# Window sums kept in one range of 128 PSUM columns, two windows to a bank, in a graph layer on one core

## The chip, the core and the metric

The kernel runs on one core of a Trainium2 chip. The core has a matmul engine (PE; its weight loads appear as PEld), a vector engine (DVE), a scalar engine (ACT), GpSimd (POOL) and SyncE (SP), which issues most of the DMAs. They work side by side, each through its own list of instructions in order, and wait for each other by semaphores. Matmuls write into PSUM, which has eight banks of 512 float32 columns for each of 128 partitions; DVE and ACT read it from there. The metric is the device time of one execution in microseconds, lower is better.

## The reference

A graph layer with a residual and a layer norm over 6250 nodes of 128 features and 100,000 edges that are sorted by destination:

```python
Xs = X[src]
m_data = Xs @ W_data.T + b_data
m_ctrl = Xs @ W_control.T + b_control
msg = jnp.where((edge_types == 0)[:, None], m_data, m_ctrl)
agg = jax.ops.segment_sum(msg, dst, num_segments=X.shape[0])
out = jax.nn.relu(agg + (X @ W_self.T + b_self))
x = layernorm(x + out)          # per node, eps 1e-5
```

Source and destination of an edge are random; on average 16 edges end in a node.

## The kernel before

**The table.** A message depends on the source node and the edge type alone. So the kernel first computes both products for all nodes: 49 blocks of 128 nodes times two types give 98 tables of 128 rows. The float32 values are split into three bfloat16 parts whose sum is nearly exact, side by side in 384 columns (`m3`, 128 x 98 x 384). This runs in 25 steps of two blocks (lines 485 to 520): a bias matmul (L499), two float32 matmuls (L502), ACT writes the first part (L507), a matmul with minus the identity takes it out of PSUM (L510), ACT or DVE writes the second part (`evict`), and DVE subtracts to get the third (L514). The blocks of transposed x come by DMA (`load_x`, L479); seven steps are loaded ahead, the others after the first part of an earlier step. `m3` is also stored to DRAM as `table`.

**The windows.** The first 6240 nodes are 39 windows of 160. A window's edges lie close together in the sorted list. A group of windows (one, two, then nine times four) is prepared in `ranks`: its edges are loaded, each edge gets a place in a list of slots, sorted by table (L702 to L779), and the lists go through DRAM (`packed`) and come back as a broadcast over 128 partitions (`rows`, L927). To find an edge's rank within its table, triangular matmuls write into a PSUM bank named `rk` (L713, L738; `ga` for the first group), and DVE takes the maximum of each row (L744). There is one such bank, so PE and DVE take turns in it.

**The sums.** `sums` then does for each window 25 groups of four tables. Stage one (L956): DVE has turned the list into 0/1 columns (L935), and four matmuls, each on 32 columns of the array, fetch 32 messages from each table: a bank `g` of 128 slots by 384 columns, with three banks in turn. ACT or DVE casts it to bfloat16 (`gs`, L444 or L445). Stage two (L970, L973): a 0/1 matrix `hot2` (DVE, L943) maps the 128 slots to the 160 nodes of the window. Four matmuls over 384 columns add the three parts, still side by side, into `a[:, :384]` for the first 128 nodes; three more, over 128 columns each, one for each part, add the other 32 nodes into `a[:, 384:]`, on three different ranges of 32 partitions. `a` has two banks. In group 12 the nodes' own product is added (`own`, L527, L530). At the end of a window ACT reads the last 128 columns (`bs`), and DVE adds the three ranges of 384 columns into `s` (L570).

**The end.** `close` adds x after the ReLU (L579) and does the layer norm for a group of windows. The ten nodes that are left are done by `gathered`: two indirect DMAs on POOL fetch their rows of `table`, and matmuls sum them in the bank `ga`.

**The order.** It is written out by a planner (`Plan`): each operation has an engine, or two to choose from, a planned duration (`act(cols)`, `dve(cols)`, constants for PE), a due time, and what it reads and writes. `Plan.run` goes through time and gives each free engine the ready operation that is due first; the instructions are then issued in that order. Buffers of one name form a ring: a user of the next buffer waits for all users of the one that it takes over. The planner's times only fix the order; on the chip semaphores decide.

PSUM before: `vt` 1 bank, `rk` 1, `ga` 1, `a` 2, `g` 3.

## Time and profile before

| | |
|---|---|
| time, median of 3 runs | 645.41 us (641.18 to 647.32) |
| profiled execution | 644.74 us, span 642.9 us |
| PE busy | 555.6 us, 86%, 13810 matmuls, 13810 weight loads |
| DVE busy | 496.3 us, 77% |
| ACT busy | 487.6 us, 76% |
| POOL busy | 31.3 us, 5% |
| mean DMA rate | 100 GB/s |

A row of the groups gives line, engine, operation, output <- input with shapes, the count (x), then the busy time in us and the mean of one in ns, and the idle time of the engine just before with what ended it. A row of a timeline gives start and length in us; in square brackets stands the idle time before it and what ended it. "issue" is a wait for nothing that the profile shows. A row of the waits gives the total in us, the count and the longest. A row of the stretches gives the stretch, its length, the busy time and the count of instructions of an engine, the granted clock, the share of the DMA engines and GB/s. A row of the DMA queues gives packets, MB, and the time of the packets as a share of 16 DMA engines' time.

### The profile page before, as it was taken

How to read it: one execution, taken by the hardware profiler on the slowest of the kernel's cores; microseconds unless marked ns; L12 is line 12 of the kernel's file. 1: busy time of each engine (PE TensorE's matmuls, PEld its weight loads, DVE VectorE, ACT ScalarE, POOL GpSimd, SP SyncE). 2: the span in 40 equal slices, each digit the busy share in tenths (PEclk: the TensorE clock that was granted, in tenths of full speed). 3: DMA queues.
4: the chain of work that ended last, by engine and by line, in shares of the span. 5: the costliest groups of instructions: out<-in, count | busy, mean ns of one | idle time of the engine just before them, and what ended most of it. 6: DMA issues, size and time to landing. Idle time of an engine off the chain costs nothing.

```text
span 642.9 us, 32170 instructions
## 1 busy us (share of the span) xinstructions
PE 555.6 (86%) x13810; PEld 427.6 (67%) x13810; DVE 496.3 (77%) x1502; ACT 487.6 (76%) x1258; POOL 31.3 (5%) x32
## 2 busy tenths in 40 slices
PE   5878789459989989898998899889889988989992
PEld 3544567338868777776787687678768767766771
DVE  6679688948988898788699979879987988685411
ACT  3545678348879787787888788888889788778992
POOL 1000100100010001001000100100010010010000
PEclk9989899759999999999999999999999999999997
DMA  3895821162045105403520630351253054022300
GB/s 109 244 303 160 246 58 50 22 188 80 3 125 153 44 33 181 107 6 125 135 63 29 188 106 4 125 165 32 73 147 94 5 185 104 17 90 95 82 16 15
DMA packets 56060, 64.33 MB, mean 100 GB/s; under 512 B 18159, under 2 KB 47828, under 8 KB 55908
## 3 DMA queue, kind: packets, MB, share of 16 engines
q1 hardware_dynamic: 54417, 59.68, 31.0%
q0 software_dynamic: 1120, 2.23, 1.6%
q8 instruction: 110, 1.80, 1.2%
q14 instruction: 43, 0.34, 0.2%
q10 hardware_dynamic: 370, 0.26, 0.2%
HBM read 45.94 MB, written 14.30 MB: 94 GB/s over the span
## 4 chain that ended last, share of the span: by engine, by line
PE 68%; ACT 12%; DVE 7%; DMA 5%; issue 5%; SPq 1%; another core or an unknown queue 0%; ACTq 0%; POOLq 0%; DVEq 0%
PE a L970 24%; PE g L956 23%; ACT gs L444 7%; PE rk L738 5%; PE a L973 5%; PE vt L775 3%; ACT to_d L451 3%; DMA hots<-past 2%; PE rk L713 1%; DVE slot L744 1%; PE g L502 1%; PE a L527 1%; DMA rows<-packed 1%; DVE rows L935 1%; PE vt L862 1%
## 5 line engine op out<-in xcount | busy, mean ns | idle before, releaser
L444 ACT CAST gs<-g 128x384 bf16<-128x384 f32 x927 | 391.8, 483 | 85.4 <-PE g L956 69.1
L956 PE MATMUL g<-m,rows 128*32 128x384 bf16 x3822 | 364.1, 331 | 14.0 <-DVE rows L935 8.4
L970 PE MATMUL a<-gs,hot 128*32 128x384 bf16 x3744 | 341.8, 333 | 34.1 <-ACT gs L444 21.0
L956 PEld LDWEIGHTS <-rows 128*32 128x32 bf16 x3822 | 250.4, 134 | 26.5 <-DVE rows L935 9.5
L970 PEld LDWEIGHTS <-hot 128*32 128x32 bf16 x3900 | 172.7, 95 | 103.7 <-issue 61.9
L973 PE MATMUL a<-gs,hot 128*32 128x128 bf16 x2808 | 231.9, 220 | 0.3 <-issue 0.3
L744 DVE TENSOR_REDUCE slot<-rk 124x4 f32<-124x392 f32 x209 | 117.4, 562 | 49.3 <-PE rk L738 42.8
L973 PEld LDWEIGHTS <-hot 128*32 128x32 bf16 x2925 | 116.7, 97 | 8.4 <-issue 4.6
L943 DVE TENSOR_TENSOR hot<-iota_b,to_d 128x1280 bf16<-128x1280 bf16 (+1 forms) x117 | 95.7, 841 | 0.0
L738 PE MATMUL rk<-hots,tri 128*32 128x392 bf16 (+1 forms) x880 | 86.1, 324 | 9.5 <-DMA hots<-past 5.3
L702 DVE TENSOR_TENSOR hots<-iota_b,st 124x784 bf16<-124x784 bf16 (+2 forms) x120 | 58.6, 506 | 4.9 <-PE vt L775 4.9
L935 DVE TENSOR_SCALAR rows<-rows,pid 128x1568 bf16<-128x1568 bf16 x78 | 46.9, 622 | 16.2 <-DMA rows<-packed 16.1
L738 PEld LDWEIGHTS <-tri 128*32 128x32 bf16 x968 | 38.4, 96 | 18.6 <-issue 13.5
L884 POOL DMA_INDIRECT sr<-table,at x20 | 25.9, 1293 | 476.4 <-DVE to_d L877 425.6
L570 DVE TENSOR_REDUCE s<-a 128x128 f32<-128x384 f32 x39 | 21.7, 556 | 34.6 <-PE a L973 22.9
L775 PEld LDWEIGHTS <-two 124*64 124x64 bf16 x858 | 21.7, 110 | 12.2 <-DVE two L766 5.9
L775 PE MATMUL vt<-hots,two 124*64 124x98 bf16 x836 | 26.1, 210 | 3.4 <-DVE two L766 1.7
L451 ACT COPY to_d<-vs 32x100 bf16<-32x100 bf16 (+3 forms) x84 | 22.2, 265 | 1.3
L760 DVE TENSOR_TENSOR hr<-slot_f,slot 124x768 bf16<-124x768 bf16 (+2 forms) x39 | 20.2, 517 | 2.6 <-ACT slot L448 2.6
L444 ACT CAST gl<-g 64x384 bf16<-64x384 f32 x39 | 18.4, 472 | 4.7 <-PE g L956 4.7
L713 PE MATMUL rk<-hots,later 124*32 124x392 bf16 (+1 forms) x210 | 20.8, 335 | 0.8 <-DVE slot L744 0.8
L766 DVE TENSOR_TENSOR two<-hr,lo 124x768 bf16<-124x768 bf16 (+2 forms) x39 | 20.2, 517 | 0.1
(188 smaller groups left out, 502.1 us busy)
## 6 DMA issues: line engine op xcount, KB each, us to landing
rows<-packed SPq DMA_DIRECT2D x39, 784.0 KB
table<-m SPq DMA_DIRECT2D x12, 768.0 KB
xc<-in_xt SPq DMA_DIRECT2D x9, 320.0 KB
rows<-in_xt SPq DMA_DIRECT2D x8, 256.0 KB
xr<-in_x SPq DMA_DIRECT2D x8, 256.0 KB
out<-xr SPq DMA_DIRECT2D x8, 256.0 KB
gl<-sr SPq DMA_DIRECT2D x39, 48.0 KB
win<-in_edges SPq DMA_DIRECT2D x38, 32.0 KB
```

The costliest lines, as they stand in the source:

```text
L444: [("ACT", act(cols), lambda: A.copy(o(), src())), ("DVE", dve(cols), lambda: V.tensor_copy(o(), src()))], None, None, due, r, w, lat)
L451: "ACT", 0.1 + cols / 1000, lambda: A.copy(o(), src()), due, r, w)
L702: lambda k=k, kn=kn, ci=ci, hs4=hs4: V.tensor_tensor(hv(ci)[:EP, k - KS[ci] : k - KS[ci] + kn].rearrange("p k w (c d) -> p (k w) c d", d=2 ...
L713: T.matmul(cnt.t[R * j : R * j + R, :wide], later.t[:EP, R - 1 - k : 2 * R - 1 - k], flat(k, EP), start=k < 4, stop=k + 4 > KT - 2, skip_g ...
L738: T.matmul(acc.t[R * j : R * j + R, (k - k0) * wide : (k - k0 + 1) * wide], tri.t[:, R * j : R * j + R], flat(k, P), start=k == k0, stop=True,
L744: vec(due, (k1 - k0) * wide, lambda k0=k0, k1=k1, acc=acc: V.tensor_reduce(slot.t[:, k0:k1, :], acc.t[:EP, : (k1 - k0) * wide].rearrange(" ...
L775: T.matmul(vv()[q : q + 64, i // 2, :], two.t[:EP, (k - k0) * nw + i].rearrange("p f r -> p (f r)"), one(k)[:EP, i, :], start=k == 0 and i ...
L935: add("DVE", dve(half * NT, 0.335), lambda sp=sp, rs=rs: V.tensor_scalar(sp.t[:, rs], sp.t[:, rs], pid1.t, None, op0=ALU.is_equal), due - ...
L943: lambda i=i, hot2=hot2, s4=s4, c0=c0, c1=c1: V.tensor_tensor(hot2.t[:, c0:c1].rearrange("p g (c d) -> p g c d", d=2), iota1_b.t.rearrange ...
L956: T.matmul(gp.t[R * t : R * t + R, :D3], sp.t[:, :, 4 * g + t], m3.t[:, 4 * g + t, :], start=True, stop=True)
L970: T.matmul(a.t[R * j : R * j + R, :D3], hot2.t[:, g, R * j : R * j + R], gs.t, start=g == 0, stop=False, skip_group_check=True)
L973: T.matmul(a.t[R * c : R * c + R, D3:], hot2.t[:, g, P:], gs.t[:, c * D : (c + 1) * D], start=False, stop=last, skip_group_check=True)
```

## The change

The three parts of a window's sum are added in the same 128 columns: stage two has twelve matmuls over 128 columns (three parts times four ranges of 32 nodes) and the three for the other 32 nodes as before. A sum now takes 256 columns, and two windows share one bank, `ab` (class `Half`). [...] `close` feeds the sum straight from PSUM to the ReLU step; the reduction into `s` stays for the ten gathered nodes alone.

The banks that are freed go to `rk`, which has two and serves the first group and the gathered nodes too, and to `g`, which has four. The table's products use `g` alone. In every second step of the table the third part comes from a second matmul with minus the identity and an eviction, not from DVE's subtraction, and the second part is always ACT's. All loads of x are issued without waiting for a step. The gathered nodes are planned 260 planned us later. Planned durations of ACT and of some matmuls change.

PSUM after: `vt` 1 bank, `rk` 2, `ab` 1, `g` 4.

```diff
+class Half(Buf):
+    @property
+    def t(self):
+        return self.base.t[:, self.turn]
...
             for i, b in enumerate(ring):
+                b.turn = i % b.bufs
...
 def act(cols):
-    return 0.055 + cols / 1200
+    return 0.12 + cols * 0.00085
...
+    banks = Buf(plan, ps, [P, 2, 256], F32, "ab", 1)
+    turn = Buf(plan, None, None, None, "turn")
+
+    def sums_bank():
+        b = Half(plan, None, None, None, "a", 2)
+        b.base = banks
+        return b
...
-    G0, G1 = 0.0, -4
+    G0 = 20
...
-    def load_x(q, after):
+    def load_x(q):
         if q in loads:
             c, i, j, q0 = loads[q]
             add("SP", SPD, lambda: S.dma_start(
                 xf(c)[:, i * P : j * P], xt[:, q0 * P : (q0 + j - i) * P]),
-                4.0 + MS * q - 9, after, [(xts[c], i)], lat=3.0)
-    AHEAD = 7
-    for q in range(AHEAD):
-        load_x(q, [])
+                -9.0 + 0.5 * q, [], [(xts[c], i)], lat=3.0 + 0.6 * q)
+    for q in range(NS):
+        load_x(q)
...
-        mp = B(ps, [P, 512], F32, *(("a", 2) if q % 5 > 2 else ("g", 3)))
+        mp, half = B(ps, [P, 512], F32, "g", 4), 0
...
-            add("PE", 0.5 if i else 0.71, product, due + 0.5 * i, [xk, w_sb, one3, brows], [mp])
+            add("PE", 0.43 if i else 0.64, product, due + 0.5 * i, [xk, w_sb, one3, brows], [key])
...
-        evict(lambda mv3=mv3: mv3(1), pv3, n, due + 1.8, [mp], [(m3, (q, 1))])
-        add("DVE", dve(n), lambda pv3=pv3, mv3=mv3: V.tensor_sub(mv3(2), pv3(), mv3(1)),
-            due + 2.4, [mp, (m3, (q, 1))], [(m3, (q, 2))])
+        add("ACT", act(n), lambda pv3=pv3, mv3=mv3: A.copy(mv3(1), pv3()), due + 1.8, [key],
+            [(m3, (q, 1))])
+        if q % LOP:
+            add("DVE", dve(n), lambda pv3=pv3, mv3=mv3: V.tensor_sub(mv3(2), pv3(), mv3(1)),
+                due + 2.4, [key, (m3, (q, 1))], [(m3, (q, 2))])
+        else:
+            add("PE", 0.11 * nb, lambda f=less_part: f(1), due + 2.4, [minus, (m3, (q, 1))], [key])
+            evict(lambda mv3=mv3: mv3(2), pv3, n, due + 3, [key], [(m3, (q, 2))])
...
-                s = B(work, [P, D], F32, "s", 3)
-                vec(da, D3 + 70, lambda a=a, s=s, m=m: V.tensor_reduce(
...
+                got, src = a, lambda a=a, m=m: a.t[:m, :D]
+                if tag:
+                    s = B(work, [P, D], F32, "s", 1)
...
-        bank = "rk" if gi else "ga"
-        cnt = B(ps, [P, 512], F32, bank, 1)
+        cnt = B(ps, [P, 512], F32, "rk", 2)
...
-            acc = B(ps, [P, 512], F32, bank, 1)
+            acc = B(ps, [P, 512], F32, "rk", 2)
...
-            a = B(ps, [P, 512], F32, "a", 2)
+            a = sums_bank()
...
-                gp = B(ps, [P, 512], F32, "g", 3)
+                gp = B(ps, [P, 512], F32, "g", 4)
...
-                    for j in range(4):
-                        T.matmul(a.t[R * j : R * j + R, :D3], hot2.t[:, g, R * j : R * j + R],
-                                 gs.t, start=g == 0, stop=False, skip_group_check=True)
                     for c in range(3):
-                        T.matmul(a.t[R * c : R * c + R, D3:], hot2.t[:, g, P:],
+                        for j in range(4):
+                            T.matmul(a.t[R * j : R * j + R, :D], hot2.t[:, g, R * j : R * j + R],
+                                     gs.t[:, c * D : (c + 1) * D], start=g == 0 and c == 0,
+                                     stop=False, skip_group_check=True)
+                    for c in range(3):
+                        T.matmul(a.t[R * c : R * c + R, D:], hot2.t[:, g, P:],
                                  gs.t[:, c * D : (c + 1) * D], start=False, stop=last,
                                  skip_group_check=True)
-                add("PE", 0.22, stage2, d + 0.9, [gs, (hot2, (g >= 9) + (g >= 17))], [a])
+                add("PE", 0.23, stage2, d + 0.9, [gs, (hot2, (g >= 9) + (g >= 17))] + (
+                    [turn] if g else []), [a] if g else [a, turn])
...
-            ga = B(ps, [P, 512], F32, "ga", 1)
+            ga = B(ps, [P, 512], F32, "rk", 2)
...
-    g0, g1 = T0 + G0, T0 + (NW + G1) * TW
-    step = max((g1 - g0) / max(sum(GT), 20), GC + 0.02)
+    g0, step = T0 + G0 * TW, GC + 0.02
```

## The prediction

> **What bounds the kernel now.** I read the page first: the busy times, the DMA queues and the chain that ended last.

> ```profile
> PE 555.6 (86%) x13810; PEld 427.6 (67%) x13810; DVE 496.3 (77%) x1502; ACT 487.6 (76%) x1258; POOL 31.3 (5%) x32
> q8 instruction: 110, 1.80, 1.2%
> PE 68%; ACT 12%; DVE 7%; DMA 5%; issue 5%; SPq 1%; another core or an unknown queue 0%; ACTq 0%; POOLq 0%; DVEq 0%
> ```

> PE carries two thirds of the chain; ACT and DVE are busy nearly as long. To see where a window's time goes I split the span at the reads of the window sums: window 3 is read at 151.70 us, window 38, the last, at 629.7. After that read and the group of all of them come the matmuls (x) in the stretch before it and in the middle, then the waits of the middle.

> ```profile
> 151.70 0.56 DVE L570 TENSOR_REDUCE s<-a 128x128 f32<-128x384 f32 x1
> L570 DVE TENSOR_REDUCE s<-a x39: 547/558/559, 89.8 to 629.7; 128x128 f32<-128x384 f32 x39
> 61.00:151.70 90.70, 67.59 (x1517) 0.83 0.37 103
> 151.70:629.70 478.00, 438.93 (x11871) 1.00 0.30 87
> ACT gs L444 <- PE g L956: 53.1, 67, 3.0
> DVE slot L744 <- PE rk L738: 34.3, 47, 1.5
> PE a L970 <- ACT gs L444: 17.4, 38, 1.5
> PE a L970 <- issue: 7.2, 8, 1.3
> PE vt L775 <- issue: 1.7, 1, 1.7
> ```

> The middle is 35 windows in 478.0 us, 13.66 each, with PE busy 92% of it. Each window runs 11871/35 = 339 matmuls, each with its own weight load (equal counts on the page). Next the timeline inside a dense stretch:

> ```profile
> 301.60 0.35 PE L970 MATMUL a<-gs,hot 128*32 128x384 bf16 x4
> 301.76 0.24 PE L973 MATMUL a<-gs,hot 128*32 128x128 bf16 x3
> 301.78 0.38 PE L956 MATMUL g<-m,rows 128*32 128x384 bf16 x4
> 301.99 0.35 PE L970 MATMUL a<-gs,hot 128*32 128x384 bf16 x4
> ```

> One group of slots takes 0.39 us: 11 matmuls and 11 weight loads. Then the waits "issue", in which PE waits for no semaphore. Two of them in the timeline, the matmul counts between four such stalls (211.53, 269.01, 311.12, 545.94), and the instruction queue in windows of 0.1 us at 266.8, 270.1, 308.8 and 312.3:

> ```profile
> 269.01 0.41 PE L775 MATMUL vt<-hots,two 124*64 124x98 bf16 x9 [1.66 <-issue]
> 311.12 0.32 PE L956 MATMUL g<-m,rows 128*32 128x384 bf16 x1 [0.84 <-issue]
> 211.53:269.01 57.48, 51.86 (x1408) 1.00 0.31 91
> 269.01:311.11 42.10, 37.94 (x1023) 1.00 0.29 89
> 311.12:545.94 234.82, 216.64 (x5886) 1.00 0.32 94
> q8 instruction: 1, 0.02, 60.1%
> q8 instruction: 1, 0.02, 87.9%
> q8 instruction: 1, 0.02, 60.9%
> q8 instruction: 1, 0.02, 89.8%
> 305.45:311.11 5.66, 3.63 (x129) 1.00 0.79 230
> ```

> So a block cannot follow the one before it faster than 1.2 (asking) + 1.12 (the mean packet: 1.2% x 16 x 642.9 / 110) + 1.25 (landing to running) = **3.6 us**. Now a dense block takes 128/11 x 0.39 = 4.5 us and the mean block of the middle 478/(11871/128) = 5.15 us. The fetch is hidden, with under 1 us to spare where PE is dense.

> **The change, part by part.** *The sum in one range of 128 columns.* For each group, four matmuls over 384 columns become twelve over 128; the three over 128 stay. Streaming is the same: a quarter of PE's array (32 of its columns) still runs 384 + 128 columns. What is added is 8 matmuls and 8 weight loads in each of 25 groups, 200 pairs for a window. Would the array keep up? The nearest row is the scatter:

> ```profile
> 324.34 0.71 PE L775 MATMUL vt<-hots,two 124*64 124x98 bf16 x24
> 324.98 0.35 PE L970 MATMUL a<-gs,hot 128*32 128x384 bf16 x4
> ```

> 24 matmuls of 98 columns, each with a weight load, in two halves of the array: 0.64 us, 27 ns each with the start, so 53 ns per half for 98 columns (41 ns of streaming at the pace of 384 columns in 0.16 us). Weight loads hide there, and a group costs 0.39 to 0.40 us in the array as before. But 19 pairs in 0.39 us use up a block of 128 pairs in 2.6 us, and it takes 3.6 us to bring one. Per window: (339 + 200)/128 = 4.21 blocks, at 3.6 us 15.2 us against 13.66 now.

> To that come late packets. The middle stretch has 11871/128 = 93 blocks and nine exposed stalls in the rows above; the late packet lost 3.3 - 1.2 = 2.1 us. If only those nine were late, 0.2 us per block. If the broadcast that each window needs holds one of its 4.2 blocks each time, 0.5:

> ```profile
> rows<-packed SPq DMA_DIRECT2D x39, 784.0 KB
> ```

> I take 0.4, nearer to the second, since a denser PE asks more often while a broadcast runs: a block every 4.0 us, 16.8 us per window.

> The stalls put borders at 256 instructions and show a wait one block after a late packet. [...]

> *The bank shared by two windows.* The reads of one window's sum now share a bank with PE's writes of the next. In before two reads of one bank, of different columns, stand behind one another:

> ```profile
> 618.00 0.56 DVE L570 TENSOR_REDUCE s<-a 128x128 f32<-128x384 f32 x1 [7.60 <-PE a L973]
> 618.59 0.26 ACT L444 COPY bs<-a 96x128 f32<-96x128 f32 x1 [0.27 <-DVE s L570]
> L579 DVE SCALAR_TENSOR_TENSOR xr<-s,xr 128x128 f32<-128x128 f32 x39 | 11.1, 284 | 0.1
> L579 DVE SCALAR_TENSOR_TENSOR xr<-vt,xr 128x128 f32<-128x128 f32 (+1 forms) x10 | 2.9, 286 | 0.2
> L943 DVE TENSOR_TENSOR hot<-iota_b,to_d 128x1280 bf16<-128x1280 bf16 (+1 forms) x117 | 95.7, 841 | 0.0
> ```

> ACT waits for DVE although neither writes. So I expect PE's next second-stage matmuls to wait for both reads: 0.26 + 0.29 us and three hand-overs of 0.03, less a first stage of 0.16 that can go between, about 0.5 us a window; 1.3 if DVE is in one of its 0.84 us masks. Behind the waiting matmul stand the first stages and rank products; ACT's evictions and DVE's slot maxima wait for those. The block time covers it: PE needs 2.6 of each 3.6 us. Without that cover it costs 18 to 45 us in all.

> *The reduction goes.* 39 x 0.556 = 21.7 us leave DVE; the ReLU step reads PSUM at the same price (284 against 286 ns). DVE is not what ends a window, so I count 0.3 us at the last one. A half is now held until the rows of x are there; they are asked for 20 us ahead.

> *Four slot banks, two rank banks, new planner costs.*

> ```profile
> L444 ACT CAST gs<-g 128x384 bf16<-128x384 f32 x927 | 391.8, 483 | 85.4 <-PE g L956 69.1
> ```

> They attack the three waits above: at most (53.1 + 34.3 + 17.4)/35 = 3.0 us per window, on three engines at once. While blocks arrive every 4 us they are not what is late, so nothing. ACT being priced dearer moves more evictions to DVE, 0.48 us each on ACT, into the time freed there.

> *The lead-in.*

> ```profile
> 24.65 0.16 DVE L1010 TENSOR_TENSOR t_rel<-t_raw,gbase 128x2 f32<-128x2 int32 x1 [3.80 <-DMA t_raw<-in_edges]
> 44.21 0.52 PE L738 MATMUL rk<-hots,tri 128*32 128x196 bf16 x8 [3.42 <-DMA hots<-past]
> 127.32 9.65 DMA hots<-past
> L514 DVE TENSOR_TENSOR m<-g,m 128x512 bf16<-128x512 f32 x15 | 10.3, 685 | 4.3 <-ACT m L444 4.3
> ```

> The gathered nodes move 260 planned us later with all they issue: the load and the two gathers on POOL's queue (POOL is busy 31.3 us in all), SP's loads and store, small DVE steps with one mask and one reduction, two matmuls and the own product. The 3.8 us stall of DVE goes; in the window loop those steps lie beside PE. All loads of x go out first on SP; four of them now stand ahead of the first window's edges. 13 of 25 third parts go from DVE (0.69 us) to a PE matmul and an eviction; the table's products get four banks instead of five. The first window starts 0 to 6 us sooner. What really holds window 3 is the ranks of its group, whose chain ends in the 9.65 us DMA. A second rank bank shortens it; PE's slower blocks lengthen it: windows 0 to 2 and the ranks ran 1517 pairs up to 151.7, now 2300, 18 blocks or 72 us of 91. Bounds -25 and +13 us; I take -8.

> **The sum**, against the profiled execution's 644.74 us (span 642.9, 1.84 around it; the median of the runs is 645.41, 0.1% above): 151.7 - 8 = 143.7, plus 35 x 16.8 = 588, plus the end 644.74 - 629.7 = 15.0 less 0.3: **746 us**. Low: 127 + 35 x 15.2 + 14.5 = 674. High: 165 + 35 x (4.21 x 4.1 = 17.3) + 15 = 785.

> **The rivals.** *The fetch stays hidden; faster.* If blocks are asked for sooner when PE uses them faster, nothing adds to PE, and the banks do their work: half of the rank and evictions waits of PE and DVE, (34.3 + 17.4)/2/35 = 0.74 us, and 0.28 for the shorter read, less 0.5 for the bank: 13.15 us a window, 143.7 + 460 + 14.7 = **618 us**. It decides from a turn-round under 2.6 us. For it: the stalls cost only 7.2 + 1.7 us in 478 now. Against: the packets after both stalls came 1.2 us after PE went on, never sooner. 12%.

> *No fetch bound, and the bank waits outweigh the gains*: if a mask of DVE stands in front of its read each time, 1.3 us a window against half of 1.02, 13.66 + 0.8 = 14.46 us, 143.7 + 506 + 14.7 = **664 us**. 5%. Something between these two, within 1%: 5%.

> *Weight loads bind in the array*:

> ```profile
> L970 PEld LDWEIGHTS <-hot 128*32 128x32 bf16 x3900 | 172.7, 95 | 103.7 <-issue 61.9
> ```

> 95 ns each, four per quarter and group instead of 512 columns' 0.21 us of streaming, +0.17 us x 25 = 4.2 us a window, 143.7 + 35 x 17.9 + 14.7 = **785 us**. The scatter, a matmul with its load every 53 ns per half, speaks against it. 3%.

> *The forecast*: 75%.

> **How the numbers follow.** 746 is the forecast's sum. Its own bounds, 674 to 785, hold nine tenths of 75%; with the loads' rival and the 664 that is 76%, and the part of the within-1% case above 650 brings it near 8 in 10. So 650 to 785. About 1% is what a measurement of this kernel can tell from no change. Faster 12%, same 5%, slower 83%.

> **What would show it.** The instruction queue has about (13810 + 7800)/128 = 169 packets; "issue" leads PE's waits with over 100 us, in stalls of about 1 us, 128 pairs apart; windows are 16 to 17.5 us apart; ACT and DVE fall below 70% busy. I am wrong in the step "one block ahead" if blocks of 128 pairs follow within 3 us; wrong in the late packets if windows take 15.2; wrong about the bank if no PE wait names the reads of the sum.

## The result and the profile after

The changed kernel takes 735.86 us against 643.91 us for the kernel before, both medians of four runs taken side by side: a ratio of 1.142, with a 95% interval of 1.136 to 1.149. The forecast was 746 us. The profiled execution took 736.92 us.

First the page of the changed kernel: the busy times, the instruction queue and the chain that ended last by engine.

```profile
PE 582.2 (79%) x21623; PEld 487.2 (66%) x21623; DVE 493.7 (67%) x1515; ACT 477.2 (65%) x1206; POOL 26.6 (4%) x32
q8 instruction: 171, 2.80, 1.6%
PE 70%; issue 15%; ACT 7%; DVE 4%; DMA 2%; another core or an unknown queue 0%; SPq 0%; ACTq 0%; DVEq 0%
```

Every engine is busy for a smaller share of the time than before, and "issue", 5% of the chain before, is 15%. PE has 7,813 more matmuls and is busy 27 us longer; the kernel takes 92 us longer. So most of the new time is time in which PE does nothing.

Next the pace of the windows. DVE's reduction, by which the prediction timed them, is gone, so both traces are now read at ACT's eviction of a window's 32 nodes (bs). In the trace of before that of window 3 is here:

```profile
151.40 0.27 ACT L444 COPY bs<-a 96x128 f32<-96x128 f32 x1
```

In the changed kernel it is at 137.12 us, and the last one at 723.59. The first row below is the group of these evictions (ACT has 38 of the 39), the second the stretch from window 3 to window 38: its ends, its length, PE's busy time with its matmuls, the clock, the DMA share and the GB/s.

```profile
L459 ACT COPY bs<-ab x38: 261/261/262, 83.0 to 723.6; 96x128 f32<-96x128 f32 x38
137.12:723.59 586.47, 466.99 (x18886) 0.99 0.24 72
```

35 windows take 586.47 us, 16.76 each instead of 13.66, with 18886/35 = 540 pairs each instead of 339. PE is busy 80% of the stretch, 92% before. Divided by 128 the matmuls make 147.5 blocks, one every 3.98 us.

The waits in this stretch (total, times, longest):

```profile
ACT gs L459 <- PE g L980: 142.9, 161, 3.6
DVE slot L768 <- PE rk L762: 80.7, 76, 3.5
PE ab L995 <- issue: 53.4, 72, 3.5
PE g L980 <- issue: 19.6, 31, 1.5
PE ab L999 <- issue: 11.6, 12, 2.5
PE ab L995 <- ACT gs L459: 10.1, 17, 1.2
PE ab L995 <- ACT bs L459: 7.7, 17, 0.6
PE ab L995 <- DVE xr L604: 4.0, 8, 0.5
```

PE's three largest waits name no semaphore: 84.6 us, where the rows of before had 7.2 and 1.7. ACT and DVE wait for PE more than twice as long as before (53.1 and 34.3), PE less for ACT (17.4). The two last rows are the shared bank: PE stands still for the reads of the sum, 11.7 us in all.

Last, the block borders. Three consecutive stretches from one stall to the next, then two rows of the timeline at such a stall, then the instruction queue in the 0.1 us from 159.7 and from 163.5 us.

```profile
158.67:162.40 3.73, 3.15 (x129) 1.00 0.02 4
162.40:166.13 3.73, 3.11 (x129) 1.00 0.02 4
166.13:169.86 3.73, 3.31 (x130) 1.00 0.02 4
165.12 0.39 PE L995 MATMUL ab<-gs,hot 128*32 128x128 bf16 x10
166.13 0.23 PE L995 MATMUL ab<-gs,hot 128*32 128x128 bf16 x2 [0.62 <-issue]
q8 instruction: 1, 0.02, 68.8%
q8 instruction: 1, 0.02, 75.1%
```

Here hardly anything else is on the DMA engines (share 0.02), and PE still stops every 128 pairs, once in 3.73 us, in the middle of a group of twelve matmuls (ten before the stall, two after). The packets last 1.10 and 1.20 us. The first ends at about 160.85 and PE goes on at 162.40; the next starts 1.1 us after that, ends at about 164.7, and PE goes on at 166.13. The turn-round is 1.1 + 1.15 + 1.5 us.

The whole stretch shows the same borders. PE's waits for nothing that the profile shows come to 91 us there, and 84 of them end at a matmul whose number in PE's program leaves 89 to 92 when it is divided by 128 (92 early in the stretch, 89 at its end). Between neighbouring stalls of this kind lie 89 distances of 128 pairs: 22 are 3.5 us, 31 are 3.7, 14 are 4.0, only seven lie between these values, and 15 are longer. So the turn-round is not one number, and the three blocks above are of its middle kind.

### The profile page after: what moved, and what is told of

The parts are those of the page before. It is cut to its first block, busy times and chain, and to the rows that moved or that the text cites. A ratio compares the mean times of both kernels' runs of the same rounds, so it can differ in the third digit from the quotient of the medians.

```text
span 735.2 us, 47681 instructions
## 1 busy us (share of the span) xinstructions
PE 582.2 (79%) x21623; PEld 487.2 (66%) x21623; DVE 493.7 (67%) x1515; ACT 477.2 (65%) x1206; POOL 26.6 (4%) x32
## 4 chain that ended last, share of the span: by engine, by line
PE 70%; issue 15%; ACT 7%; DVE 4%; DMA 2%; another core or an unknown queue 0%; SPq 0%; ACTq 0%; DVEq 0%
PE ab L995 27%; PE g L980 22%; PE ab L999 6%; PE rk L762 4%; PE vt L799 3%; ACT gs L459 3%; PE g L519 2%; ACT to_d L466 2%; PE ab L550 1%; DVE xr L604 1%; ACT bs L459 1%; PE rk L737 1%; PE vt L886 1%; PE g L526 1%; DMA past<-csb 1%
## 5 line engine op out<-in xcount | busy, mean ns | idle before, releaser
L459 ACT CAST gs<-g 128x384 bf16<-128x384 f32 x896 | 376.5, 489 | 172.6 <-PE g L980 155.6
L995 PE MATMUL ab<-gs,hot 128*32 128x128 bf16 x11232 | 382.4, 222 | 82.8 <-issue 54.8
L995 PEld LDWEIGHTS <-hot 128*32 128x32 bf16 x11700 | 337.0, 97 | 128.1 <-issue 112.9
L980 PE MATMUL g<-m,rows 128*32 128x384 bf16 x3822 | 370.7, 340 | 26.6 <-issue 21.8
L999 PE MATMUL ab<-gs,hot 128*32 128x128 bf16 x2808 | 251.0, 221 | 12.3 <-issue 12.0
L980 PEld LDWEIGHTS <-rows 128*32 128x32 bf16 x3822 | 202.4, 135 | 46.2 <-issue 39.7
L768 DVE TENSOR_REDUCE slot<-rk 124x4 f32<-124x392 f32 (+2 forms) x214 | 118.1, 562 | 94.3 <-PE rk L762 88.5
L999 PEld LDWEIGHTS <-hot 128*32 128x32 bf16 x2925 | 135.0, 98 | 13.4 <-issue 13.4
L604 DVE SCALAR_TENSOR_TENSOR xr<-ab,xr 128x128 f32<-128x128 f32 x39 | 11.4, 291 | 87.7 <-PE g L980 37.4
L459 ACT COPY bs<-ab 96x128 f32<-96x128 f32 x38 | 9.9, 261 | 39.1 <-PE ab L999 16.2
L460 DVE CAST gs<-g 128x384 bf16<-128x384 f32 x40 | 21.9, 549 | 3.6 <-PE g L980 3.6
L519 PE MATMUL g<-w_sb,rows 128*128 128x256 f32 x72 | 23.3, 426 | 0.0
## 6 DMA issues: line engine op xcount, KB each, us to landing
rows<-packed SPq DMA_DIRECT2D x39, 784.0 KB
```

What stands on the lines that cost most here:

```text
L459: [("ACT", act(cols), lambda: A.copy(o(), src())), ("DVE", dve(cols), lambda: V.tensor_copy(o(), src()))], None, None, due, r, w, lat)
L519: T.matmul(mt()[:, 256 * i : 256 * i + 256], xf(c)[:, k * P : k * P + P], w_sb.t[:, : 2 * D], start=False, stop=False, skip_group_check=True)
L768: vec(due, (k1 - k0) * wide, lambda k0=k0, k1=k1, acc=acc: V.tensor_reduce(slot.t[:, k0:k1, :], acc.t[:EP, : (k1 - k0) * wide].rearrange(" ...
L980: T.matmul(gp.t[R * t : R * t + R, :D3], sp.t[:, :, 4 * g + t], m3.t[:, 4 * g + t, :], start=True, stop=True)
L995: T.matmul(a.t[R * j : R * j + R, :D], hot2.t[:, g, R * j : R * j + R], gs.t[:, c * D : (c + 1) * D], start=g == 0 and c == 0, stop=False, ...
L999: T.matmul(a.t[R * c : R * c + R, D:], hot2.t[:, g, P:], gs.t[:, c * D : (c + 1) * D], start=False, stop=last, skip_group_check=True)
```

## The experiments

**Only the instructions.** The rival causes of the lost time are the fetch, the shared bank, and the weight loads in the array. This kernel has the split alone.

```diff
-                    for j in range(4):
-                        T.matmul(a.t[R * j : R * j + R, :D3], hot2.t[:, g, R * j : R * j + R],
-                                 gs.t, start=g == 0, stop=False, skip_group_check=True)
+                    for c in range(3):
+                        for j in range(4):
+                            T.matmul(a.t[R * j : R * j + R, c * D : (c + 1) * D],
+                                     hot2.t[:, g, R * j : R * j + R],
+                                     gs.t[:, c * D : (c + 1) * D], start=g == 0 and c == 0,
+                                     stop=False, skip_group_check=True)
```

> The kernel before with one edit: the four matmuls of 384 columns become twelve of 128, each into its own third of the 384 columns. Two whole banks for the sums, the reduction, the slot and rank banks and the lead-in stay as they were. Theory of the fetch (a block of 256 PE instructions takes 3.6 us at least, 4.0 with late packets): 539 pairs a window, 4.21 blocks, 16.8 us a window instead of 13.66, 750 to 770 us in all, about 169 packets. Rival (the shared bank costs the time): 645 us, within 1%. Rival (weight loads bind in the array): 17.9 us a window, no stalls at every 128 pairs.

Measured: 753.46 us, ratio 1.171 (1.162 to 1.180). Its instruction queue and its stretch from window 3 to window 38:

```profile
q8 instruction: 170, 2.79, 1.5%
155.92:740.84 584.92, 476.23 (x18876) 0.98 0.25 73
```

16.71 us a window, as in the changed kernel, with no shared bank and none of its other edits, and 80 of PE's 84 us of stalls without a semaphore lie at the block borders again. The added instructions explain the whole loss within the windows; by itself this run does not tell the fetch from the array.

**Half of them.** Each wide matmul is cut into 256 and 128 columns.

```diff
+                    for c0, c1 in ((0, 2 * D), (2 * D, D3)):
+                        for j in range(4):
+                            T.matmul(a.t[R * j : R * j + R, c0:c1],
+                                     hot2.t[:, g, R * j : R * j + R],
+                                     gs.t[:, c0:c1], start=g == 0 and c0 == 0,
+                                     stop=False, skip_group_check=True)
```

> The kernel before with each matmul of 384 columns cut in two (256 and 128), so 8 in place of 4: half of the added instructions. Theory of the fetch: (339 + 100)/128 = 3.43 blocks a window, at 3.6 to 4.0 us 12.3 to 13.7 us, which lies beside the 13.66 us that a window takes now: 645 to 665 us, so far less than half of the full split's price. Rival (every added pair costs the same, about 15 ns): half of the full price, about 700 us. Rival (weight loads bind in the array, 2.75 loads of 95 ns per quarter and group against 0.21 us of streaming): +1.3 us a window, 690 us.

Measured: 683.35 us, ratio 1.064 (1.057 to 1.070). That is 41 us for half of the instructions, and 111 for all: less than half of it, but more than I had expected. The stretch, and a dense block inside it with the stall that ends it:

```profile
150.97:663.87 512.90, 457.78 (x15376) 0.98 0.28 82
199.28:203.01 3.73, 3.54 (x128) 1.00 0.40 88
203.01 0.39 PE L956 MATMUL g<-m,rows 128*32 128x384 bf16 x3 [0.19 <-issue]
```

My expectation set 3.43 blocks of 4.0 us beside the 13.66 us of a window, that is, beside a mean. But where PE is dense it has 3.54 us of work in a block that comes after 3.73, and is held: the packets of the stretch start 3.77 us apart in the median, 4.73 in the kernel before. The time in which PE waits for ACT or DVE comes on top (for ACT's casts alone 22.5 us in the span). A window takes 14.65 us. The fetch has to be compared with the dense stretches.

Late packets are the other part. Stalls at block borders come to 27 us in this stretch, and ten of them, 2.0 to 2.8 us each, make 23. Their packets start 2.6 to 4.3 us after the border instead of 1.1, and in that time the DMA engines' share is 0.82 to 1.00.

The weight loads' rival, 690 us, lies close too; against it stand PE's stalls at the block borders, those 27 us, and the run without broadcasts below.

**Without the sharing.** The changed kernel with each window's sum in a bank of its own, and three slot banks.

```diff
-        b = Half(plan, None, None, None, "a", 2)
-        b.base = banks
-        return b
+        return B(ps, [P, 512], F32, "a", 2)
...
-                gp = B(ps, [P, 512], F32, "g", 4)
+                gp = B(ps, [P, 512], F32, "g", 3)
```

> The changed kernel with the twelve narrow matmuls into the same 128 columns kept, but each window's sums in a bank of its own (two whole banks), paid with three slot banks instead of four. Theory of the fetch: 16.8 us a window as before it, 730 to 745 us, within 1% of the changed kernel; the waits of PE for the reads of the sum go. Rival (the shared bank costs 0.5 to 1.3 us a window on the path): 690 to 718 us.

Measured: 731.65 us, ratio 1.138 (1.132 to 1.144), 0.6% below the changed kernel, with a ratio inside that kernel's interval. A window takes 16.58 us:

```profile
134.20:714.42 580.22, 469.85 (x18908) 0.98 0.25 74
```

The waits of PE for the reads of the sum are gone and almost nothing is gained. The shared bank was covered by the fetch.

**Without the broadcasts.** The changed kernel, with the rows that each window compares kept from the first one, so that 38 of 39 broadcasts go.

```diff
-            for j in range(RP):
+            for j in range(RP if w0 + i == 0 else 0):
...
-                    sp.t[:, rs], sp.t[:, rs], pid1.t, None, op0=ALU.is_equal), due - 4 + q,
+                    sp.t[:, rs], rows1.t[:, rs], pid1.t, None, op0=ALU.is_equal), due - 4 + q,
```

> The changed kernel with the rows of packed slots broadcast to all partitions once, for the first window, and kept: every window compares with that copy (each later window leaves out its own rows, 784 KB of broadcast); two buffers fewer for gathered messages make the room. All else, the instructions of PE too, stays. My step on late packets says that a broadcast holds one of a window's 4.2 blocks by about 2 us, 0.4 us a block on the mean: without it a block comes every 3.6 us, a window takes 15.2 us instead of 16.76, and with window 3 read near 130 us it is 130 + 35 x 15.2 + 14 = 676 us (660 to 695). Rival (the packets are late for other reasons, such as PE being held by the other engines between blocks): 16.2 to 16.8 us a window, 710 to 735 us.

Measured: 697.27 us, ratio 1.086 (1.079 to 1.092).

```profile
130.80:684.43 553.63, 462.30 (x18890) 0.99 0.12 30
```

PE's program is the same (18890 pairs in the stretch, 18886 in the changed kernel), and the kernel is 39 us faster with the DMA share at 0.12 instead of 0.24: what PE waits for goes through the DMA engines. An array that cannot keep up would not have gained. A window takes 15.82 us and a block 553.63/(18890/128) = 3.75 us. So the broadcasts cost 0.23 us a block, not 0.4, and the time lies between the theory's 660 to 695 us and the rival's 710 to 735. The 3.75 that are left are a mean: of 75 distances between neighbouring stalls at the borders, 33 are 3.5 us, 31 are 3.7 or 3.8 and 11 are 4.0 or more. What makes the longer ones was not looked into by a run.

**The count by itself.** I tried to add instructions that use neither array nor bank, in two ways. First empty ones, 16 and 32 a group:

```diff
+                    for k in range(16):
+                        T.nop(nofuse=True)
```

> The kernel before with 16 instructions that do nothing put into PE's program behind the four wide matmuls of each group: as many instructions as the full split adds, but no matmul, no weight load, no bank and no wait. Theory of the fetch: 1078 instructions a window, 4.21 blocks of 256, 16 to 17 us a window, 740 to 770 us, about 169 packets, stalls at block borders. Rival (the added matmuls or weight loads cost the array or the weight port): 645 us, within 1%. Rival (PE's sequencer pays for each instruction whatever it fetches, more than 20 ns for an empty one): PE's gaps of that size inside every group and more than 770 us.

> The same with 32 empty instructions in each group. Theory of the fetch: 1478 instructions, 5.77 blocks a window; at the 3.6 to 4.0 us of a block 20.8 to 23.1 us a window, about 160 + 35 x 22 + 15 = 945 us (900 to 985), about 230 packets. Rival (the price is not one of blocks): no multiple of the price of 16.

They measured 643.22 us (ratio 1.002, 0.999 to 1.005) and 644.88 us. The page of the first, as that of the second, shows why they say nothing:

```profile
q8 instruction: 110, 1.80, 1.2%
```

110 packets as before: the program that PE fetched was no longer than that of the kernel before, so the empty instructions were not in it. Then tests of a semaphore that is already raised, two in one instruction:

```diff
+    spare = nc.alloc_semaphore("spare")
+    T.sem_inc(spare, 1)
...
+                    for k in range(32):
+                        T.wait_ge(spare, 1)
```

> The kernel before with 16 instructions in each group that only test a semaphore which PE itself raised at the start: no matmul, no weight load, no bank, nothing to wait for. PE's program is as long as with the full split (171 blocks of 16 KB). Theory of the fetch: 16 to 17 us a window, 735 to 770 us, as the twelve narrow matmuls did (753). Rival (matmuls or weight loads are what costs): 643 us, within 1%. Rival (each test costs PE's sequencer over 25 ns by itself): windows longer than 17.5 us, with time lost inside the groups instead of at block borders.

Measured: 1918.34 us, ratio 2.985 (2.966 to 3.005), with 171 packets, 61 more than in before: at 256 instructions a packet 16 for the 32 tests of a group. The second rival holds: the time is lost at the tests, not at the borders.

```profile
PE a L977 <- issue: 750.5, 964, 1.5
```

964 waits, about one for each of 975 groups, stand at the first matmul behind the 16 tests. In the trace the tests start 106 ns apart in the median, so 16 of them fill 1.7 of the 1.97 us of a group. The kernel is longer by (1918.34 - 642.75)/(39 x 25 x 16) = 82 ns for each test. The granted clock was 0.52 in this run and 0.97 in before, and a wide matmul of stage two took 521 ns instead of 333, so the 82 ns are no clean price: part of PE's work runs beside the tests (the 16 fill 1.7 us, and a group got 1.3 us longer), and that work is slower here. So the price of instructions that only have to be fetched was not isolated; the case for the fetch rests on the stalls at the borders, the split alone, its half, and the run without broadcasts.

**Without the split.** The changed kernel with four wide matmuls, two whole sums banks, the reduction, and three slot banks.

```diff
+                    for j in range(4):
+                        T.matmul(a.t[R * j : R * j + R, :D3], hot2.t[:, g, R * j : R * j + R],
+                                 gs.t, start=g == 0, stop=False, skip_group_check=True)
                     for c in range(3):
-                        for j in range(4):
-                            T.matmul(a.t[R * j : R * j + R, :D], hot2.t[:, g, R * j : R * j + R],
-                                     gs.t[:, c * D : (c + 1) * D], start=g == 0 and c == 0,
-                                     stop=False, skip_group_check=True)
...
-                got, src = a, lambda a=a, m=m: a.t[:m, :D]
+                s = B(work, [P, D], F32, "s", 3)
+                vec(da, D3 + 70, lambda a=a, s=s, m=m: V.tensor_reduce(
+                    s.t[:m], a.t[:m, :D3].rearrange("p (c d) -> p d c", c=3), axis=AX.X,
+                    op=ALU.add), [a], [s])
```

> The changed kernel with the split and the shared bank undone: four matmuls of 384 columns, two whole banks for the sums, the reduction on DVE, three slot banks instead of four. Two rank banks, the planner's costs and the lead-in stay changed. Theory of the fetch: a window takes 12.9 to 13.7 us again and window 3 is read near 137 us: 137 + 35 x 13.3 + 15 = 617 us (605 to 640), faster than both kernels. Rival (the rank banks, the planner's costs or the lead-in slow the window): it stays above 660 us.

Measured: 617.01 us, ratio 0.958 (0.952 to 0.963): faster than both kernels.

```profile
131.62:603.63 472.01, 437.30 (x11903) 0.99 0.30 89
```

A window takes 13.49 us, little less than the 13.66 of before. Most of the gain, 20 us, lies ahead of window 3, read at 131.62 instead of 151.40. The split, with the shared bank and the fourth slot bank that go with it, had taken 3.3 us a window and 5.5 us of the lead-in.

The same without the reduction:

```diff
-                s = B(work, [P, D], F32, "s", 3)
-                vec(da, D3 + 70, lambda a=a, s=s, m=m: V.tensor_reduce(
-                    s.t[:m], a.t[:m, :D3].rearrange("p (c d) -> p d c", c=3), axis=AX.X,
-                    op=ALU.add), [a], [s])
+                got, src = a, lambda a=a, m=m: a.t[:m, :D]
```

> The kernel without the split (four wide matmuls, two whole sums banks, three slot banks, two rank banks) that leaves the reduction out: the ReLU step takes the first 128 columns alone, so two thirds of a sum are left out. My step says that the 0.56 us of the reduction are beside the path, 0.3 us in all at the end: 614 to 618 us against 617. Rival (a window's end waits for the reduction, 0.28 to 0.56 us each): 595 to 607 us.

Measured: 616.38 us, ratio 0.960 (0.955 to 0.965). What the change set out to remove was worth 0.6 us, which two such runs do not tell from nothing. This kernel and the one with the split in two whole banks differ by the narrow matmuls alone: its windows take 13.56 us against 16.58, and its window 3 is read at 128.07 us against 134.20. So the split costs 3.0 us a window and 6.1 us of the lead-in by this pair.

**Where the lead-in's gain comes from.** First the kernel without the split with one rank bank and four slot banks.

```diff
-        cnt = B(ps, [P, 512], F32, "rk", 2)
+        cnt = B(ps, [P, 512], F32, "rk", 1)
...
-                gp = B(ps, [P, 512], F32, "g", 3)
+                gp = B(ps, [P, 512], F32, "g", 4)
```

> The kernel without the split (four wide matmuls, two whole banks for the sums, the changed lead-in and planner's costs) with four slot banks and one rank bank in place of three and two. My step on the lead-in says that the second rank bank shortens the chain of the ranks that window 3 waits for: without it window 3 is read later than 131.6 us, by some 3 to 10 us, and the total is 617 to 630 us. Rival (the lead-in's gain comes from the loads of x and the moved gathered nodes alone): window 3 read at 132 us within 2, and with a fourth slot bank 605 to 617 us.

Measured: 632.83 us, ratio 0.982 (0.975 to 0.990), above my 617 to 630 and far above the rival's 605 to 617. Its profiled execution, 637.6 us, was the longest of its four, so it is read only roughly: window 3 came at about 147 us, 15 later than with two rank banks where I had said 3 to 10, and one wait led PE's:

```profile
PE rk L757 <- DMA hots<-past: 22.2, 6, 11.3
```

So I took the second bank for the cause and put it alone into the kernel before:

```diff
-        bank = "rk" if gi else "ga"
+        bank = "rk"
-        cnt = B(ps, [P, 512], F32, bank, 1)
+        cnt = B(ps, [P, 512], F32, bank, 2)
...
-            ga = B(ps, [P, 512], F32, "ga", 1)
+            ga = B(ps, [P, 512], F32, "rk", 2)
```

> The kernel before with one edit: the counts and rank products of all groups and the gathered nodes share two rank banks, where the first group and the gathered nodes had a bank of their own and the other groups one. By the run with one rank bank (window 3 read at 146.6 us against 131.6 with two) the second bank brings window 3 about 15 us forward: 137 us, and 625 to 631 us in all. Rival (loads of x and the moved gathered nodes carry the lead-in's gain): window 3 at 149 to 152 us, 640 to 645 us.

Measured: 630.07 us, ratio 0.982 (0.977 to 0.988). The total is the one I gave, for another reason than I gave. The stretch from window 3, the waits within it, and two rows of the timeline before it:

```profile
149.57:613.99 464.42, 435.13 (x11870) 1.00 0.30 90
ACT gs L444 <- PE g L956: 46.7, 76, 4.3
DVE slot L744 <- PE rk L738: 25.8, 34, 2.5
PE a L970 <- ACT gs L444: 13.9, 32, 1.4
78.91 0.33 PE L1057 MATMUL rk<-t_msg,t_hot 128*32 128x384 bf16 x1
80.72 0.35 PE L738 MATMUL rk<-hots,tri 128*32 128x392 bf16 x4 [0.18 <-DMA hots<-past]
```

Window 3 is hardly earlier. What is shorter is the window: 13.27 us, with the three waits down by 18.4 us from the 104.8 of before. Ahead of window 3 the gathered nodes' product has a rank bank from 78.9 us, and after the four rank products at 80.7 none follows until 104 us. So I moved the gathered nodes as well, and nothing else:

```diff
-    g0, g1 = T0 + G0, T0 + (NW + G1) * TW
-    step = max((g1 - g0) / max(sum(GT), 20), GC + 0.02)
+    g0, step = T0 + G0 * TW, GC + 0.02
```

> The kernel before with two edits: two rank banks shared by all, and the gathered nodes moved 260 planned us later as in the changed kernel. With the rank banks alone window 3 was read at 149.6 us, and no rank product ran from 81 to 104 us; the gathered nodes' product (78.9 to 80.2 us) had one of the two banks just then. Theory (with the gathered nodes out of the lead-in both banks serve the ranks of windows 3 to 6): window 3 read at 132 to 140 us, and with the 13.27 us a window of that run 136 + 35 x 13.27 + 15 = 615 us (608 to 622). Rival (the early loads of x, the third parts and the planner's costs carry it): window 3 at 146 to 150 us, 626 to 632 us.

Measured: 615.18 us, ratio 0.965 (0.962 to 0.969).

```profile
131.00:599.76 468.76, 437.00 (x11901) 1.00 0.30 89
```

Window 3 at 131.0: the two edits together bring the whole gain of the lead-in. The rank banks alone did not bring it (149.57). The gathered nodes were not moved alone; moved with the rest of the changed lead-in, but with one rank bank, they left window 3 at about 147 us. The loads of x, the third parts and the planner's costs are not needed for it. In the run before this one DVE's reduction of the gathered nodes' sum comes only at 105.29 us, and PE's rank product at 105.88 waits for it: that sum held one of the two rank banks for 27 us. No run separates this from the gathered nodes' other work. With no split this kernel too beats both kernels.

## Why the prediction was right

*One block ahead, 3.6 us at least.* Right. PE stops at every 128 pairs, packets start 1.1 us after it goes on, and the same instructions cost the same in a kernel without the other edits (16.71 us a window, 16.76 with them). Over the 115 stalls at borders the medians are 1.14 us to the packet, 1.09 for the packet and 1.40 from landing to running, 3.63 us where the sum had 1.2 + 1.12 + 1.25 = 3.57. "At least" was a little too strong: the shortest blocks took 3.45 us. In the stretch from window 3 a packet started sooner than 1.0 us after PE went on at one of these stalls only, 0.68 us after it.

*200 more pairs a window, the array keeping up.* 540 pairs were run against 539 predicted. I took 2.6 us of PE's work for a block; its busy time in the three blocks shown is 3.1 to 3.3 us, ranks and scatters included. The margin was thinner than I said, but positive.

*Late packets, 0.4 us a block.* The sum of floor and lateness, 3.98 us, came out as the 4.0 predicted, and 16.76 us a window as the 16.8. That it fits so closely is partly luck: the broadcasts are 0.23 us and not 0.4, and blocks without them still take 3.75 us on the mean and not 3.6. The two misses cancel here. They do not in the run without broadcasts, which came out at 697 us, above its 660 to 695.

*The shared bank, 0.5 us a window under the cover of the block time.* Right: 0.33 us a window on PE (11.7/35), and in all 4 us or nothing when it is taken away.

*The reduction, 0.3 us in all.* Right: 0.6 us or nothing. The ReLU step takes 291 ns from PSUM, where it took 284 from `s`.

*Slot banks, rank banks, planner's costs: nothing while blocks come every 4 us.* Right in the changed kernel: the waits that they attack grew, and a window takes 16.76 us against 16.71 with the split alone. With the fetch out of the way the rank banks are worth 0.39 us a window, 0.27 with the gathered nodes moved.

*The lead-in, 8 us sooner.* The direction was right and the size was not: window 3's eviction was read at 137.1 us, 14.3 sooner than in before. The step named the second rank bank; what it missed is that the bank acts only with the gathered nodes out of the way, and then brings 20 us. Of these PE's slower blocks take 5.5 back (4.5 and 6.1 in the two other pairs of kernels that differ by the narrow matmuls).

*The end.* 736.92 - 723.59 = 13.3 us, 14.7 predicted. The differences of the sum's three terms, in the order of time, are -6.6, -1.5 and -1.4 us, and these make the 9.5 us between 746.4 and 736.9.

*The rivals.* The 618 us of the first are close to what the kernel takes when the split is left out (617), but that is luck. That run has neither the shared bank nor the fourth slot bank; its windows take 13.49 us and not 13.15, and its window 3 comes at 131.6 us and not 143.7. What is real in the rival is that rank banks shorten a window when the fetch does not bind (13.27 us against 13.66). The second rival has windows of 14.46 us, held up by reads of the shared bank; they took 16.76, and without the sharing still 16.58. In the array's rival windows take 17.9 us and do not mind the broadcasts; they took 16.76, and 15.82 without the broadcasts.

*What would show it.* 171 packets for 169; windows of 16.76 us; ACT and DVE at 65% and 67%. "Issue" leads PE's waits, with 84.6 us in the three rows of the stretch, where I had said over 100; the chain puts 15% of 735.2, 110 us, down to it.

## What to carry to other kernels

Count the instructions as well as the columns: here the next 128 matmuls with their weight loads mostly came 3.5 to 3.7 us after the last 128, so cutting matmuls into narrower ones, with the same columns streamed, cost 3.1 us a window. Compare that time with the densest stretch, not with the mean of a loop: half of the cut already cost 41 us, a part of it by late packets, though the mean seemed to leave room. And before a step is bought off an engine, see what the kernel gains when the step is simply left out: here 0.6 us.

## What the hardware showed that I had not expected

- The tests of a semaphore that was already raised, two to an instruction, started 106 ns apart on PE in the median; 975 groups of 16 made the kernel 1276 us longer, 82 ns for each, at a granted clock of 0.52.
- The turn-round of an instruction block fell mostly on 3.5, 3.7 or 4.0 us (22, 31 and 14 of 89) and seldom between (3.73 in three blocks with the DMA engines nearly idle, share 0.02), and the window's broadcasts added 0.23 us to each block on the mean although the instruction queue moved only 2.8 MB.
- The half split put PE's dense block (3.54 us of work) almost exactly on that turn-round, so that kernel sat 0.2 us from it with little on its page that said so; "issue" in the chain was 5% in before, 7% there and 15% with the full split.
